# A gather-and-multiply graph layer: leftover rows placed in wider tiles, and the first 128 columns multiplied from a resident tile

## The chip, the cores and the metric

The kernel runs on one core of a Trainium2 chip. The metric is the time of one execution in microseconds (us), measured on the device; lower is better. The engines are named as the profile names them: PE (matmul), PEld (loading of PE's weights), DVE (VectorE), ACT (ScalarE), POOL (GpSimd), SP (SyncE).

## The reference

One layer of a graph network with a residual and a normalisation. The adjacency matrix is sparse in its far columns and nearly full in its first ones, because an entry is present with a probability that falls as the root of both indices.

```python
B, N, F_IN, F_OUT = (8, 4096, 256, 256)
HW = jnp.einsum('bnf,fo->bno', H, W)               # H is x
A_norm = jax.nn.relu((A + A.T) * 0.5)
D = jnp.sum(A_norm, axis=1)
d_inv_sqrt = jnp.where(D > 0, D_safe ** (-0.5), 0.0)
DAD = d_inv_sqrt[:, None] * A_norm * d_inv_sqrt[None, :]
L_norm = jnp.eye(N) - DAD
out = relu(jnp.einsum('nm,bmo->bno', L_norm, HW))
x = _layernorm(x + out, axis=-1)
```

All is float32.

## The kernel before

**First stage (0 to about 584 us).** The adjacency is read in squares of 512 by 512, made symmetric by PE transposes and a DVE addition (`symmetrise`, L364), passed through relu, summed for the degrees (L369) and written to `a_dram`. Beside that, `form` multiplies 128 rows of x by W, scales them and writes them to `g_dram`: a row of `g` has 8 x 256 float32 numbers, 8 KB. The first block of 128 output rows is multiplied densely here (`lead`).

**Second stage (about 584 us to the end).** The other 31 blocks of 128 output rows are worked off in 16 units of two blocks (the last unit has one), in the order `SEQ`. A unit has four quarters of 64 output rows. A column m of the adjacency touches some of the four quarters, which gives a pattern of 1 to 15: bits 1 and 2 are the two quarters of the first block (b=0), bits 4 and 8 those of the second (b=1). Only columns with a pattern above zero have to be fetched. They are sorted into tiles of 128 columns by kind: `KINDS` lists the patterns that have tiles of their own, kind 0 takes all others and whatever finds no place, and multiplies all four quarters. `CAPS[u]` says how many tiles of each kind unit u has. For a tile, `gather` issues two indirect DMAs on POOL: the 128 columns' entries of the adjacency (`ga`, L733, 512 B or 1 KB a row) and the 128 rows of `g` (L744). The `g` tiles go into a ring of `RING` buffers of 1 MB. Slots of a tile that hold no column are left out of the fetch of `g`.

PE multiplies a tile once for each 512-number bank of the output (four banks) and each block that it touches (L933). A product for one quarter uses 64 of PE's columns; two products for different halves stand side by side. `steps_of` therefore puts tiles of kinds 1 and 2, 4 and 8, 5 and 10 into one step, and mixes the (1, 2) steps with those of kind 0.

**The lists.** Which column goes where is computed on the chip, four units ahead. `patterns(u)` finds the pattern of each column (DVE). `count` multiplies by ones and by a triangle on PE, to number the columns of each kind. `place(u)` (L212) takes these numbers from PSUM, keeps those below the kind's capacity and makes slots of them (DVE, tiles of 11 kinds x 32); `place_rest` does so for kind 0. `spread` and `collect` turn slots into lists, `index` turns the lists into the addresses for the gathers. Four units' `place` runs in the first stage, from `count_place`, beside `symmetrise`, and twelve in the second.

**The order around a unit's end.** Work is written in an order made by hand: `after(n, fn)` runs a function n products later, `queue("dve")` and `in_turn` pin an instruction behind the engine's last one. When block b=0 of a unit is complete, `finish` evicts it (ACT, L620, into `y`, one buffer); one product later DVE normalises it (`moments`, `inverse_root`); two products later `lists` puts `count`, `count_rest` and `collect` on PE, into two PSUM banks with the tag `b0`; one later `read(False)` runs on DVE up to the `yield` of `index`, `place_rest` and `place`, and six later `read(True)` the rest. The tag `b0` has four banks, and the next unit's first block needs all four: its third and fourth bank are those that the lists used.

Of the kernel before, what the change touches and what calls it, by code (L numbers as in the profile page):

```python
# [16 lines left out]

KINDS = [1, 2, 3, 0, 6, 9, 5, 10, 12, 4, 8]  # L20

SEQ = [1, 2, 3, 4, 5, 6, 7, 0, *range(8, 16)]

CAPS = [
# [16 lines left out]
]  # L41


# [1 line left out]
def kernel(  # L45
# [36 lines left out]
    Q = 64  # L82
    QU = 4
    HOLD = 10
    RING = 13
    EPS = 1e-5
    NK = len(KINDS)
    tiles = [sum(caps) for caps in CAPS]
    first = [[sum(caps[:k]) for k in range(NK)] for caps in CAPS]
    mid = KINDS.index(0), KINDS.index(12)  # L90
    tmax = max(tiles)

    const = ctx.enter_context(tc.tile_pool(name="const", bufs=1))
# [83 lines left out]
    def patterns(u):  # L177

        used = ipool.tile([P, QU, NB], F32, tag="used", name=f"used_{u}", bufs=1)
        nb = blocks(u)  # L180
        if nb == 1:
            nc.vector.memset(used, 0.0)
        lo = (2 * u + 1) * 2
        nc.vector.tensor_scalar(
            used[:, : 2 * nb],
            part[:, :, lo : lo + 2 * nb].rearrange("p m s -> p s m"),
            0.0,
            None,
            ALU.is_gt,
        )  # L190
# [14 lines left out]
        plan[u] = pat, kind  # L205

    def count(u, tot, low):
        kind = plan[u][1].rearrange("p k m -> p (k m)")
        nc.tensor.matmul(tot, lhsT=ones, rhs=kind, start=True, stop=True)
        nc.tensor.matmul(low, lhsT=lower, rhs=kind, start=True, stop=True)  # L210

    def place(u, tot, low):  # L212

        pat, kind = plan[u]
        pos, _ = scan(tot, low, NK * NB, f"k{u}")
        yield
        pos = pos.rearrange("p (k m) -> p k m", k=NK)  # L220
        fits = ipool.tile([P, NK, NB], F32, tag="fits", name=f"fits_{u}", bufs=1)
        nc.vector.tensor_tensor(
            fits, pos, limit[:, u].unsqueeze(2).to_broadcast([P, NK, NB]), ALU.is_lt
        )
        nc.vector.tensor_tensor(fits, fits, kind, ALU.mult)
# [18 lines left out]
    def place_rest(u, tot, low):  # L244

        slot, rest = plan[u]
        pos, incl = scan(tot, low, NB, f"r{u}")
        yield
        room = CAPS[u][mid[0]] * P
# [3 lines left out]
        nc.vector.scalar_tensor_tensor(  # L253
            pos, pos, float(first[u][mid[0]] * P + 1), fits, ALU.add, ALU.mult
        )
# [47 lines left out]
    def index(u, pl):  # L303
        t = tiles[u]

        low = ipool.tile([P, tmax], F32, tag="low", name=f"low_{u}")
        nc.vector.tensor_copy(low[:, :t], pl[:, 1, :])
        nc.vector.scalar_tensor_tensor(low[:, :t], pl[:, 0, :], float(P), low[:, :t], ALU.mult, ALU.add)
        yield
        gi = ipool.tile([P, tmax], U32, tag="gi", name=f"gi_{u}", bufs=3)  # L310
        nc.vector.tensor_scalar(gi[:, :t], low[:, :t], float(N), None, ALU.add)

        ai = ipool.tile([P, tmax], U32, tag="ai", name=f"ai_{u}", bufs=3)
        m0, m1 = first[u][mid[0]], first[u][mid[1]]
        if blocks(u) == 1:
            m0 = m1 = t
        for ts, n, k in (
            (slice(0, m0), NB, 2 * u + 1),
            (slice(m0, m1), NU, u),
            (slice(m1, t), NB, 2 * u + 2),  # L320
        ):
            if ts.start == ts.stop:
                continue
            nc.vector.tensor_scalar(
                ai[:, ts], low[:, ts], float(n), float(N * n + k), ALU.mult, ALU.add
            )
        plan[u] = gi, ai

    def run(steps):
        for _ in steps:  # L330
# [342 lines left out]
    def targets(u, kind):  # L673

        if kind == 0:
            kind = 15 if blocks(u) == 2 else 3
        out = []
        for b in range(2):
            h = kind >> 2 * b & 3
            if h:  # L680
                out.append((b, {1: slice(0, Q), 2: slice(Q, P), 3: slice(0, P)}[h]))
        return out

    def steps_of(u):
# [12 lines left out]

    with (
# [5 lines left out]
            gath.enter_context(tc.tile_pool(name=f"gath_{k}", bufs=1)).tile([P, G], F32, name=f"g{k}")  # L704
            for k in range(RING)
        ]
        lpool = gath.enter_context(tc.tile_pool(name="spread", bufs=1))
        stat = gath.enter_context(tc.tile_pool(name="stat", bufs=3))
        steps = [(u, step) for u in SEQ for step in steps_of(u)]
# [14 lines left out]
        def gather(n):  # L724

            if n >= len(order):
                return
            u, kind, t = order[n]
            gi, ai = plan[u]
            both = len(targets(u, kind)) == 2  # L730
            at = apool.tile([P, 2 * P], F32, tag="a", name=f"ga_{u}_{t}")
            with queue("pool"):
                nc.gpsimd.indirect_dma_start(  # L733
                    out=at if both else at[:, :P],
# [4 lines left out]
                )  # L739


            gt = ring[n % RING]
            with queue("pool"):
                nc.gpsimd.indirect_dma_start(  # L744
                    out=gt,
# [268 lines left out]
```

## Time and profile before

| | |
|---|---|
| median of 14 runs | 1605.54 us (1599.77 to 1609.9) |
| profiled execution, its own time | 1601.25 us |
| its span, first to last instruction | 1599.5 us |
| granted TensorE clock, mean | 0.981 |
| PE busy | 1493.5 us, 93% |
| DVE busy | 891.6 us, 56% |
| POOL busy | 752.9 us, 47% |
| moved by DMA | 575.71 MB, mean 360 GB/s |

A group of instructions is a line of the kernel, an engine, an operation, what it writes and reads, and the count; then busy time and the mean of one in ns, and the idle time just before, with what ended it. A table of stretches gives for each engine its busy time and the number of its instructions, then the granted clock of PE, the busy share of the DMA engines and their rate.

A float32 product shows as two records, for the weights and for the matmul alike: the 1,576 products of L933 are 3,152 records on PE.

### The profile page before, as it was taken

Reading aid. Unit: us, or ns where it says so; the run is one execution under the profiler, and the core shown is the slowest. Engines: PE = TensorE matmul, PEld = TensorE weight load, DVE = VectorE, ACT = ScalarE, POOL = GpSimd, SP = SyncE. Lnnn points to the kernel's source line nnn. Section 1 sums busy time; section 2 is a strip of 40 time slices with the busy share of each in tenths; the row PEclk is TensorE's granted clock in tenths of the full one; section 3 lists DMA queues with packets and bytes.
Section 4 is the critical chain, followed back from the end, with each engine's and each line's share of the span. In section 5 each row is a group of like instructions: output and inputs, shape, how many; then the busy total and the mean of one; then the engine's idle time right before and its main releaser. Section 6 shows DMA issues by size and latency. Waiting matters only on the chain.

```text
span 1599.5 us, 18959 instructions
## 1 busy us (share of the span) xinstructions
PE 1493.5 (93%) x6544; PEld 778.9 (49%) x6544; DVE 891.6 (56%) x2250; ACT 371.3 (23%) x462; POOL 752.9 (47%) x1109
## 2 busy tenths in 40 slices
PE   6999989998889898999999999899999998999983
PEld 5787877777677643333343333334333332333331
DVE  5675678876474604446384473671176656666542
ACT  3555554554344500101001010010001101100111
POOL 3001010102122257576676676676676667666662
PEclk9999999999999999999999999999999999999998
DMA  9999999999889889999999999999999999999994
GB/s 351 376 362 406 390 374 373 397 383 367 290 325 327 344 351 401 375 404 339 399 370 370 372 369 362 379 367 370 344 351 338 345 376 365 368 387 377 350 342 159
DMA packets 222037, 575.71 MB, mean 360 GB/s; under 512 B 20403, under 2 KB 108771, under 8 KB 184195
## 3 DMA queue, kind: packets, MB, share of 16 engines
q0 software_dynamic: 59552, 316.19, 51.6%
q10 hardware_dynamic: 72032, 134.51, 22.2%
q1 hardware_dynamic: 90352, 123.74, 22.1%
q8 instruction: 54, 0.88, 0.2%
q14 instruction: 47, 0.39, 0.1%
HBM read 479.07 MB, written 136.34 MB: 385 GB/s over the span
## 4 chain that ended last, share of the span: by engine, by line
PE 66%; DMA 18%; issue 6%; DVE 5%; POOL 2%; ACT 2%; another core or an unknown queue 0%; POOLq 0%; ACTq 0%; SPq 0%; DVEq 0%
PE py L933 44%; PE pg L469 10%; DMA g<-g_dram,gi 10%; PE lead L427 5%; DMA a_dram<-sym 4%; PE xtr L458 3%; PE tr L360 3%; DVE sym L364 3%; DMA xin<-in_x_dram 2%; ACT sym L368 1%; DVE part L369 1%; POOL g L744 1%; POOL ga L733 1%; DMA xr<-in_x_dram 1%; DMA adj<-in_adj_dram 1%
## 5 line engine op out<-in xcount | busy, mean ns | idle before, releaser
L933 PE MATMUL py<-g,ga 128*64 128x512 f32 (+1 forms) x3152 | 942.6, 599 | 40.1 <-issue 19.9
L933 PEld LDWEIGHTS py<-g,ga 128*64 128x64 f32 (+1 forms) x3152 | 344.6, 153 | 626.5 <-issue 597.9
L744 POOL DMA_INDIRECT g<-g_dram,gi x302 | 335.7, 1111 | 242.9 <-issue 80.6
L733 POOL DMA_INDIRECT ga<-a_dram,ai x302 | 328.2, 1087 | 99.5 <-issue 86.2
L631 DVE TENSOR_TENSOR xr<-xr,y 128x2048 f32<-128x2048 f32 x31 | 71.2, 2296 | 446.0 <-ACT y L620 388.9
L620 ACT ACTIVATE y<-py,minus_r 128x512 f32<-128x512 f32 x120 | 81.6, 687 | 885.9 <-PE py L933 812.0
L469 PE MATMUL pg<-w_sb,xt 128*128 128x256 f32 x1024 | 230.6, 383 | 5.3 <-ACT xt L459 5.2
L364 DVE TENSOR_TENSOR sym<-tr,adj 128x512 f32<-128x512 f32 x256 | 162.9, 682 | 112.3 <-PE tr L360 95.0
L469 PEld LDWEIGHTS pg<-w_sb,xt 128*128 128x128 f32 x1024 | 194.4, 192 | 33.6 <-ACT xt L459 6.0
L369 DVE TENSOR_REDUCE part<-sym 128x32 f32<-128x2048 f32 x64 | 145.4, 2278 | 63.3 <-ACT sym L368 63.3
L360 PE MATMUL tr<-ident,adj 128*128 128x128 f32 x1024 | 136.0, 283 | 25.3 <-DVE sym L364 12.2
L389 POOL TENSOR_TENSOR r<-e,neg_half 128x4 f32<-128x4 f32 x8 | 8.3, 1039 | 315.8 <-DVE e L388 315.8
L368 ACT ACTIVATE sym<-sym 128x2048 f32<-128x2048 f32 x64 | 122.5, 1915 | 122.2 <-DVE sym L364 122.2
L360 PEld LDWEIGHTS tr<-ident,adj 128*128 128x128 f32 x1024 | 118.4, 145 | 53.3 <-DVE sym L364 24.5
L636 DVE BATCH_NORM_STATS2 stats<-xr 128x6 f32<-128x256 f32 x256 | 87.2, 411 | 19.4 <-POOL xr L631 18.3
L458 PE MATMUL xtr<-ident,xin 128*128 128x128 f32 x512 | 72.5, 286 | 16.4 <-DVE sym L364 14.0
L660 DVE TENSOR_SCALAR xr<-xr,mv,root 128x256 f32<-128x256 f32 x248 | 84.3, 411 | 0.1
L427 PE MATMUL lead<-gt,strip 128*128 128x512 f32 x176 | 82.5, 593 | 0.0
L479 ACT ACTIVATE gt<-pg,r 128x512 f32<-128x512 f32 x88 | 60.5, 687 | 76.8 <-PE pg L469 70.3
L459 ACT COPY xt<-xtr 128x512 f32<-128x512 f32 x128 | 68.4, 590 | 40.9 <-PE xtr L458 39.7
L458 PEld LDWEIGHTS xtr<-ident,xin 128*128 128x128 f32 x512 | 58.6, 145 | 34.3 <-DVE sym L364 26.0
L274 DVE TENSOR_TENSOR hot<-iota_q,at 128x1024 bf16<-128x1024 f32 x64 | 74.1, 1218 | 1.5 <-DMA a_dram<-sym 1.5
(114 smaller groups left out, 579.5 us busy)
## 6 DMA issues: line engine op xcount, KB each, us to landing
adj<-in_adj_dram SPq DMA_DIRECT2D x64, 1024.0 KB
a_dram<-sym ACTq DMA_DIRECT2D x64, 1024.0 KB
xr<-in_x_dram ACTq DMA_DIRECT2D x32, 1024.0 KB
out_dram<-xr SPq DMA_DIRECT2D x31, 1024.0 KB
xin<-in_x_dram SPq DMA_DIRECT2D x44, 512.0 KB
g_dram<-gt ACTq DMA_DIRECT2D x22, 1024.0 KB
xin<-in_x_dram POOLq DMA_DIRECT2D x20, 512.0 KB
g_dram<-held ACTq DMA_DIRECT2D x10, 1024.0 KB
```

The lines of the kernel that those rows point to most:

```text
L360: ins = nc.tensor.transpose(pt[:, c * P : (c + 1) * P], tji[:, c, a * P : (a + 1) * P], ident)
L364: nc.vector.tensor_add(sym[:, a, :], pt, tij[:, a, :])
L368: nc.scalar.activation(sym, sym, AF.Relu, scale=0.5)
L369: nc.vector.tensor_reduce(part[:, i * A : (i + 1) * A, j * S // Q : (j + 1) * S // Q], sym.rearrange("p a (c q) -> p a c q", q=Q), AX.X, A ...
L427: nc.tensor.matmul(lead[c], lhsT=strip, rhs=g[:, c * S : (c + 1) * S], start=not done, stop=len(done) == NB - 1, skip_group_check=True,)
L458: nc.tensor.transpose(pt[:, k, c, :], xin[b // H][:, b % H + k, c * P : (c + 1) * P], ident)
L469: ins = nc.tensor.matmul(pg[:, k * FO : (k + 1) * FO], lhsT=xt[:, b + k, c, :], rhs=w_sb[:, c, :], start=(c == 0), stop=(c == FC - 1),)
L636: nc.vector.bn_stats(stats[:, b, :], z[:, b, :])
L660: nc.vector.tensor_scalar(z[:, b, :], z[:, b, :], mv[:, b, 0:1], rstd[:, b : b + 1], ALU.subtract, ALU.mult,)
L733: nc.gpsimd.indirect_dma_start(out=at if both else at[:, :P], out_offset=None, in_=a_pairs if both else a_rows, in_offset=bass.IndirectOff ...
L744: nc.gpsimd.indirect_dma_start(out=gt, out_offset=None, in_=g_dram, in_offset=bass.IndirectOffsetOnAxis(ap=gi[:, t : t + 1], axis=0), boun ...
L933: last_product = nc.tensor.matmul(py[2 * u + 1 + b][c][rows, :], lhsT=at[:, off + rows.start : off + rows.stop], rhs=gt[:, c * S : (c + 1) ...
```

## The change

Two things are done at once.

1. A column of kind 1, 2, 4 or 8 (one quarter) that finds no place in the tiles of its kind is offered free places in tiles of two quarters, in three rounds (`OFFERS`): first kinds 3 and 12, then 5 and 10, then 9 and 6. Only what is left after that goes to kind 0. `place` computes for every kind how far each round reaches (`upto`) and by how much the slot number is shifted there (`off`, `step`, `way`). `KINDS` is put in another order, so that one slice serves two kinds, and `CAPS` has new numbers.
2. In the eleven units of `HUB` the first 128 columns take no part in the lists. They are a step of their own, multiplied for all four quarters from a tile `hub` that holds rows 0 to 127 of `g` and is loaded once; their adjacency entries come by a plain DMA. The ring has 12 buffers in place of 13.

In `index` the `yield` moves from before the address computations to behind them.

```diff
-KINDS = [1, 2, 3, 0, 6, 9, 5, 10, 12, 4, 8]
+KINDS = [3, 1, 2, 4, 8, 12, 5, 10, 9, 6, 0]
+ONE = slice(1, 5)
+OFFERS = [
+    (0, (1, 4), (3, 12)),
+    (0, (2, 8), (3, 12)),
+    (1, (1, 2), (5, 10)),
+    (1, (4, 8), (5, 10)),
+    (2, (1, 2), (9, 6)),
+    (2, (4,), (6,)),
+    (2, (8,), (9,)),
+]
+HUB = {0, 1, 3, 6, *range(8, 15)}
 CAPS = [
-    [4, 3, 2, 7, 1, 2, 2, 1, 1, 3, 3],
+    [2, 3, 3, 3, 2, 1, 2, 1, 2, 1, 6],
...
-    [3, 3, 1, 1, 1, 1, 1, 1, 1, 3, 3],
+    [1, 2, 2, 2, 2, 1, 1, 1, 1, 1, 1],
...
-    RING = 13
+    RING = 12
...
     def patterns(u):
...
+        if u in HUB:
+            nc.vector.memset(pat[:, :1], 0.0)
...
     def place(u, tot, low):
         pat, kind = plan[u]
-        pos, _ = scan(tot, low, NK * NB, f"k{u}")
+        pos, incl = scan(tot, low, NK * NB, f"k{u}")
         yield
         pos = pos.rearrange("p (k m) -> p k m", k=NK)
+        n = ONE.stop - ONE.start
+        nc.vector.tensor_copy(total, incl.rearrange("p (k m) -> p k m", k=NK)[:, :, NB - 1])
+        nc.vector.tensor_tensor(free, total, limit[:, u], ALU.min)
+        nc.vector.tensor_add(free, free, base[:, u])
+        nc.vector.tensor_tensor(total, total, limit[:, u], ALU.max)
+        nc.vector.tensor_add(ends, base[:, u], limit[:, u])
+        nc.vector.tensor_copy(upto[:, 0], limit[:, u, ONE])
+        nc.vector.tensor_copy(off[:, 0], base[:, u, ONE])
+        for s, ones_, twos in OFFERS:
+            k, t = at_once(*ones_), at_once(*twos)
+            c = slice(k.start - ONE.start, k.stop - ONE.start, k.step)
+            nc.vector.tensor_sub(off[:, s + 1, c], free[:, t], upto[:, s, c])
+            nc.vector.tensor_sub(upto[:, s + 1, c], ends[:, t], off[:, s + 1, c])
+            nc.vector.tensor_tensor(upto[:, s + 1, c], upto[:, s + 1, c], total[:, k], ALU.min)
+            nc.vector.tensor_add(free[:, t], upto[:, s + 1, c], off[:, s + 1, c])
+        nc.vector.tensor_copy(upper, limit[:, u])
+        nc.vector.tensor_copy(upper[:, ONE], upto[:, 3])
         nc.vector.tensor_tensor(
-            fits, pos, limit[:, u].unsqueeze(2).to_broadcast([P, NK, NB]), ALU.is_lt
+            fits, pos, upper.unsqueeze(2).to_broadcast([P, NK, NB]), ALU.is_lt
         )
+        nc.vector.tensor_sub(step, off[:, 1:], off[:, :3])
+        for s in range(3):
+            more = way if s == 0 else ipool.tile([P, QU, NB], F32, tag="used", name=f"more_{u}_{s}", bufs=1)
+            nc.vector.tensor_tensor(
+                more, pos[:, ONE], upto[:, s].unsqueeze(2).to_broadcast([P, n, NB]), ALU.is_ge
+            )
+            nc.vector.tensor_tensor(
+                more, more, step[:, s].unsqueeze(2).to_broadcast([P, n, NB]), ALU.mult
+            )
+            if s > 0:
+                nc.vector.tensor_add(way, way, more)
+        nc.vector.tensor_add(pos[:, ONE], pos[:, ONE], way)
...
     def index(u, pl):
...
-        yield
         gi = ipool.tile([P, tmax], U32, tag="gi", name=f"gi_{u}", bufs=3)
...
         plan[u] = gi, ai
+        yield
...
         few, all_rows = groups[:2]
+        all_rows += [[(0, -1)]] * (u in HUB)
...
         def gather(n):
...
+            if t < 0:
+                if not hub_loads:
+                    with queue("pool"):
+                        hub_loads.append(nc.gpsimd.dma_start(hub, g_dram[:P, :]))
+                with queue("pool"):
+                    nc.gpsimd.dma_start(at, a_dram[:P, (2 * u + 1) * P : (2 * u + 3) * P])
+                got[u, t] = (at, hub)
+                return
...
+            n = len(ring_tiles)
             gt = ring[n % RING]
+            ring_tiles.append(gt)
```

More of the change, by code (lines that the diff above doesn't have):

```diff
@@ L89 @@
     first = [[sum(caps[:k]) for k in range(NK)] for caps in CAPS]
-    mid = KINDS.index(0), KINDS.index(12)
+    mid = KINDS.index(4), KINDS.index(5)
     tmax = max(tiles)
@@ L210, in count, with at_once @@
         nc.tensor.matmul(low, lhsT=lower, rhs=kind, start=True, stop=True)
+    def at_once(*kinds):
+        at = [KINDS.index(k) for k in kinds]
+        return slice(at[0], at[-1] + 1, at[-1] - at[0] or 1)
     def place(u, tot, low):
         pat, kind = plan[u]
-        pos, _ = scan(tot, low, NK * NB, f"k{u}")
+        pos, incl = scan(tot, low, NK * NB, f"k{u}")
         yield
         pos = pos.rearrange("p (k m) -> p k m", k=NK)
+        n = ONE.stop - ONE.start
+        total = ipool.tile([P, NK], F32, tag="total", name=f"total_{u}", bufs=1)
+        nc.vector.tensor_copy(total, incl.rearrange("p (k m) -> p k m", k=NK)[:, :, NB - 1])
+        free = ipool.tile([P, NK], F32, tag="free", name=f"free_{u}", bufs=1)
+        nc.vector.tensor_tensor(free, total, limit[:, u], ALU.min)
+        nc.vector.tensor_add(free, free, base[:, u])
+        nc.vector.tensor_tensor(total, total, limit[:, u], ALU.max)
+        ends = ipool.tile([P, NK], F32, tag="ends", name=f"ends_{u}", bufs=1)
+        nc.vector.tensor_add(ends, base[:, u], limit[:, u])
+        upto = ipool.tile([P, 4, n], F32, tag="upto", name=f"upto_{u}", bufs=1)
+        nc.vector.tensor_copy(upto[:, 0], limit[:, u, ONE])
+        off = ipool.tile([P, 4, n], F32, tag="off", name=f"off_{u}", bufs=1)
+        nc.vector.tensor_copy(off[:, 0], base[:, u, ONE])
[6 more added lines that the diff above has]
+            nc.vector.tensor_add(free[:, t], upto[:, s + 1, c], off[:, s + 1, c])
+        upper = ipool.tile([P, NK], F32, tag="upper", name=f"upper_{u}", bufs=1)
+        nc.vector.tensor_copy(upper, limit[:, u])
+        nc.vector.tensor_copy(upper[:, ONE], upto[:, 3])
@@ L221, in place @@
         fits = ipool.tile([P, NK, NB], F32, tag="fits", name=f"fits_{u}", bufs=1)
         nc.vector.tensor_tensor(
-            fits, pos, limit[:, u].unsqueeze(2).to_broadcast([P, NK, NB]), ALU.is_lt
+            fits, pos, upper.unsqueeze(2).to_broadcast([P, NK, NB]), ALU.is_lt
         )
+        step = ipool.tile([P, 3, n], F32, tag="step", name=f"step_{u}", bufs=1)
+        nc.vector.tensor_sub(step, off[:, 1:], off[:, :3])
+        way = ipool.tile([P, n, NB], F32, tag="way", name=f"way_{u}", bufs=1)
@@ L248, in place_rest @@
         yield
-        room = CAPS[u][mid[0]] * P
+        room = CAPS[u][KINDS.index(0)] * P
         nc.vector.tensor_scalar(over[:, u : u + 1], incl[:, NB - 1 : NB], float(room), None, ALU.is_gt)
@@ L253, in place_rest @@
         nc.vector.scalar_tensor_tensor(
-            pos, pos, float(first[u][mid[0]] * P + 1), fits, ALU.add, ALU.mult
+            pos, pos, float(first[u][KINDS.index(0)] * P + 1), fits, ALU.add, ALU.mult
         )
@@ L318, in index @@
             (slice(0, m0), NB, 2 * u + 1),
-            (slice(m0, m1), NU, u),
-            (slice(m1, t), NB, 2 * u + 2),
+            (slice(m0, m1), NB, 2 * u + 2),
+            (slice(m1, t), NU, u),
         ):
@@ L706 @@
         ]
+        hub = gath.enter_context(tc.tile_pool(name="hub", bufs=1)).tile([P, G], F32, name="g_hub")
+        hub_loads = []
+        ring_tiles = []
         lpool = gath.enter_context(tc.tile_pool(name="spread", bufs=1))
@@ L728, in gather @@
             u, kind, t = order[n]
+            both = len(targets(u, kind)) == 2
+            at = apool.tile([P, 2 * P], F32, tag="a", name=f"ga_{u}_{t % tmax}")
+            if t < 0:
[6 more added lines that the diff above has]
+                return
             gi, ai = plan[u]
-            both = len(targets(u, kind)) == 2
-            at = apool.tile([P, 2 * P], F32, tag="a", name=f"ga_{u}_{t}")
             with queue("pool"):
```

28 rows, old and new, of the table CAPS are left out of this document.

## The prediction

> **What bounds the kernel now.** I read the page's head first, then the chain of work that ended last, then the stretches cut at the units' ends, then the groups of instructions, and last the order of time around one unit's end.
>
> ```profile
> PE 1493.5 (93%) x6544; PEld 778.9 (49%) x6544; DVE 891.6 (56%) x2250; ACT 371.3 (23%) x462; POOL 752.9 (47%) x1109
> ...
> PE 66%; DMA 18%; issue 6%; DVE 5%; POOL 2%; ACT 2%; another core or an unknown queue 0%; POOLq 0%; ACTq 0%; SPq 0%; DVEq 0%
> ...
> 0.00:584.00 584.00, 535.97 (x2896) 418.57 (x2898) 362.07 (x529) 282.05 (x330) 91.38 (x508) 0.98 0.97 360
> 584.00:1582.00 998.00, 957.53 (x3650) 360.35 (x3646) 523.97 (x1701) 84.56 (x125) 655.88 (x596) 0.99 0.97 365
> ```
>
> The second stage takes 998 of 1599.5 us; PE is busy for 957.5 us of it and the DMA engines are 97% busy at 365 GB/s. So two resources are nearly full, and DVE (524 us) and POOL (656 us) are not.
>
> How long PE needs for a step is seen from the weight loads and from the evictions of a last step:
>
> ```profile
> 1267.47 0.14 PEld L933 LDWEIGHTS py<-g,ga 128*64 128x64 f32 x2 [0.29 <-issue]
> 1267.90 0.14 PEld L933 LDWEIGHTS py<-g,ga 128*64 128x64 f32 x2 [0.28 <-issue]
> 1478.88 0.69 ACT L620 ACTIVATE y<-py,minus_r 128x512 f32<-128x512 f32 x1 [31.93 <-PE py L933]
> 1481.46 0.69 ACT L620 ACTIVATE y<-py,minus_r 128x512 f32<-128x512 f32 x1 [0.17 <-PE py L933]
> ```
>
> Two 64-column loads go in every 0.43 us, so a pair of halves costs what one full product costs: 2 x 0.43 us for a bank. The first and fourth bank of a step are evicted 2.58 us apart, 0.86 us a bank. I call one step's worth for four banks a slot: 3.44 us.
>
> **The slots and the bytes.** From `CAPS` and `steps_of`, a (1, 2), (4, 8), (5, 10) step counts as many slots as its fuller half has products, kinds 3 and 12 one, a kind 0 or hub tile two (one in the unit with a single block). Before there are 259 slots in 302 tiles; after, 250 slots in 268 gathered tiles and 11 hub steps. By unit in the order worked: before 23, 20, 18, 17, 16, 16, 15, 31, 15, 14, 15, 14, 14, 13, 13, 5; after 23, 19, 18, 16, 15, 15, 14, 30, 15, 14, 14, 13, 13, 13, 13, 5. That is 9 x 3.44 = 31.0 us less of PE.
>
> ```profile
> 927.35 0.31 PE L209 MATMUL lists<-kind,ones 128*128 128x352 bf16 x1
> 928.59 1.94 PE L933 MATMUL py<-g,ga 128*64 128x512 f32 x8
> 930.00:934.00 4.00, 4.00 (x22) 1.37 (x20) 2.60 (x18) 0.00 (x0) 3.09 (x4) 1.00 1.02 392
> 938.00:942.00 4.00, 2.89 (x9) 0.88 (x11) 3.72 (x20) 0.00 (x0) 1.66 (x3) 1.00 1.00 410
> ```
>
> The 259 slots are 891 us of the 998; the lists' products, 1.24 us in each of 14 units, 17 us more; 90 us are waits. Where the DMA engines are full they move some 400 GB/s.
>
> The bytes: I counted the patterns of the reference's adjacency. Before, 33,471 rows of `g` are fetched in 38,656 slots of tiles; after, 32,174 in 34,304. In both cases the columns left over fit in kind 0, so the dense way at the kernel's end is not taken. The hub takes 1,297 rows of 8 KB out, 10.6 MB; its own load adds 1.05 MB; the `ga` rows fall from 25.8 to 25.0 MB. So 10.4 MB less, and at the 365 GB/s above 28.5 us.
>
> PE's 31.0 and the DMA's 28.5 us do not add: they are the same time seen from two nearly full resources. Per unit I took the larger of slots x 3.44 us + 1.24 us and bytes at 400 GB/s, with 4.2 MB for a unit's x and output. Before it gives 946 us, after 919 us: units 1, 3 and 0 are set by PE, the rest within 10% by either. I take -28 us.
>
> **Tail and ring.** At the end PE waits for gathers although the DMA is not full:
>
> ```profile
> 1552.00:1582.00 30.00, 21.08 (x70) 6.77 (x70) 11.35 (x42) 2.50 (x5) 11.96 (x11) 1.00 0.70 271
> 1571.10 4.61 PE L933 MATMUL py<-g,ga 128*64 128x512 f32 x16 [2.50 <-DMA g<-g_dram,gi]
> 1564.61 13.23 DMA g<-g_dram,gi
> ```
>
> A gather lands 13 us after its issue, a ring buffer comes free only when PE is done with it, and the last (4, 8) and (1, 2) steps use two tiles in 3.44 us. Before, the last such run is 6 + 9 tiles against 13 buffers; after, 4 + 9 against 12, and a hub step, which needs no ring buffer, lets the gathers run ahead by 6.9 us earlier in that unit. I take -4 us (bounds 0, the ring being shorter, and -9, the PE idle of that stretch). In all the second stage's tiles give **-32 us** (-20 to -40).
>
> POOL issues 34 tiles fewer, 34 x 2.2 us, and 12 plain DMAs more:
>
> ```profile
> L744 POOL DMA_INDIRECT g<-g_dram,gi x302 | 335.7, 1111 | 242.9 <-issue 80.6
> L733 POOL DMA_INDIRECT ga<-a_dram,ai x302 | 328.2, 1087 | 99.5 <-issue 86.2
> L417 POOL DMA_DIRECT2D xin<-in_x_dram x20 | 15.2, 760 | 102.3 <-PE xtr L458 101.6 <-issue 0.7
> ```
>
> That is -75 + 9 us on an engine with 342 us free in the stage: nothing by itself.
>
> **The price: DVE.** `place` grows by 38 operations on 1 to 12 numbers a partition (7 ahead of the offers, 7 x 4 in them, 3 behind) and 9 on 4 x 32.
>
> ```profile
> 931.12 0.17 DVE L653 TENSOR_TENSOR half<-root 128x8 f32<-128x8 f32 x1
> 931.32 0.17 DVE L654 SCALAR_TENSOR_TENSOR half<-half,rstd 128x8 f32<-128x8 f32 x1
> L225 DVE TENSOR_TENSOR fits<-fits,kind 128x352 f32<-128x352 f32 x16 | 8.4, 523 | 0.5
> L173 DVE TENSOR_TENSOR pos_r<-incl_r,lists 128x32 f32<-128x32 f32 x13 | 2.4, 187 | 0.5
> ```
>
> Small dependent ones start 0.20 us apart: 38 x 0.20 = 7.6 us. Between 187 ns for 32 numbers and 523 for 352, 128 cost about 0.29 us: 9 x 0.29 = 2.6 us. So 10.2 us for each unit, 163 us in all, on an engine that is not the bound on average. Where it falls decides.
>
> *First stage.* Four `place` run in two pairs beside `symmetrise`, with nothing in the code that pins their order there:
>
> ```profile
> 239.00:271.00 32.00, 28.14 (x41) 1.00 1.01 364
> 271.00:304.00 33.00, 25.83 (x55) 1.00 1.04 396
> 304.00:340.00 36.00, 30.86 (x55) 1.00 1.02 381
> 340.00:380.00 40.00, 27.50 (x47) 0.91 1.04 405
> ...
> 243.82 0.69 DVE L364 TENSOR_TENSOR sym<-tr,adj 128x512 f32<-128x512 f32 x1
> 244.43 0.52 DVE L222 TENSOR_TENSOR fits<-pos_k,limit 128x352 f32<-128x352 f32 x1
> 244.86 0.68 DVE L364 TENSOR_TENSOR sym<-tr,adj 128x512 f32<-128x512 f32 x1
> ```
>
> The first four rows show DVE alone (busy, instructions), then clock, DMA share and rate. The two stretches that hold the pairs have 3.9 and 5.1 us of DVE idle for 20.4 us more each; those behind have 7.2 and 12.5. If all idle time is filled, 20.4 - 11.1 and 20.4 - 17.6 are left over: 12 us. If none is, 41 us. PE's transposes wait for the additions that DVE then does later, PSUM having four banks for them, and the DMA, full at 1.02, cannot make up more than the few loads buffered. I take **+20 us**: nearer to the filled end, since the present `place` is interleaved with the additions one by one, as the last three rows show.
>
> *Second stage.* Here DVE waits once a unit, for the next eviction:
>
> ```profile
> 1229.00:1278.00 49.00, 49.00 (x223) 17.89 (x221) 34.98 (x114) 6.83 (x11) 34.16 (x31) 1.00 0.96 349
> 1263.05 2.29 DVE L631 TENSOR_TENSOR xr<-xr,y 128x2048 f32<-128x2048 f32 x1 [12.38 <-ACT y L620]
> 1273.50 0.52 DVE L174 TENSOR_TENSOR pos_k<-pos_k,lists 128x352 f32<-128x352 f32 x1
> 1276.62 0.30 DVE L324 TENSOR_SCALAR ai<-low 128x6 uint32<-128x6 f32 x3
> 1321.51 2.29 DVE L631 TENSOR_TENSOR xr<-xr,y 128x2048 f32<-128x2048 f32 x1 [21.07 <-ACT y L620]
> ```
>
> 12.4 and 21.1 us of idle cover 10.2, in units of 14 and 15 slots; the cover is gone where a unit with `place` has 13 slots. The other cover is at the unit's end. The first block's last product ends 0.7 us, one eviction, ahead of the addition at 1263.05; `place` has read its banks at 1274.0, 11.7 us later, and the moved `yield` puts the 0.3 us of the addresses and one operation of `gi` ahead of that: 12.2 us. PE comes to those banks after what is left of block b=1, the lists, and two banks of the next step. That was 4 slots + 1.24 + 1.7 = 16.7 us and becomes 13.3 us, with 3 slots, in seven of the twelve units that have `place`, and 9.8 us, with 2, in unit 11, where PE waits 2.4 us. In the seven it just suffices, and any lateness of DVE is then PE's. I take **+3 us** (0 to 25: twelve units late by 2 us).
>
> **Sum.** -32 + 20 + 3 = -9 us on the profiled execution's 1601.25 us. That lies 4.3 us under the median of the runs, so against 1605.5 it is 1596.5 us.
>
> **The rivals.**
>
> 1. *DVE in the first stage costs in full, and the end is slower.* Each place round then lasts as long as DVE's work in it: 4 x 10.2 = 41 us. With -32 and +3 that is +12 us: 1617 us. For it: DVE has 9 us free where 41 are added. Against: 20 us of idle right behind. It decides from 29 us on. Chance 0.25.
> 2. *DVE's saturation at the units' ends.* Twelve units, each with 2 us of PE's wait, are +24 instead of +3, so +12 in all: 1617 us. For it: 13.3 against 12.2 us. Against: DVE still has idle time in units of 14 slots and more. Chance 0.12.
> 3. *The lists cost nothing that lasts.* The first stage's additions find room, because PE or the DMA is awaited there anyway: 0 to +8 for the price, -32 for the tiles: 1578 us. Chance 0.23.
> 4. *DVE holds POOL, and the gathers come late.* POOL's issues are stretched where DVE reads two operands:
>
> ```profile
> 613.53 2.29 DVE L631 TENSOR_TENSOR xr<-xr,y 128x2048 f32<-128x2048 f32 x1 [57.09 <-issue]
> 613.61 3.09 POOL L744 DMA_INDIRECT g<-g_dram,gi  x1 [1.20 <-remote]
> L744 POOL DMA_INDIRECT g<-g_dram,gi x302: 999/1005/3089, 572.1 to 1564.6; - x151
> L733 POOL DMA_INDIRECT ga<-a_dram,ai x302: 940/944/3040, 567.1 to 1562.3; - x151
> ```
>
> One issue took 3.09 us where the median (the middle of each three) is 1.005. Mean less median, 0.106 and 0.143 us, times 302 each is 75 us of hold under 524 us of DVE; 122 us more of DVE would hold POOL 17 us more. If all of it falls where a gather is awaited, -9 + 17 = +8: 1613 us. Against: POOL has 342 us free. Chance 0.10. [...]
>
> The forecast itself, faster by 2 to 20 us, has 0.30.
>
> **How the numbers follow.** The forecast and rival 3 hold 0.53; with the ends of the others that pass zero, faster by over 0.2% (3.2 us, about what the runs can tell) gets 0.56, within it 0.14, slower 0.30. The range takes the tiles at their better end with rival 3's price, -40 + 8 + 0 = -32, and reaches 5 us past the slower rivals' +12: 1573 to 1622 us. The likeliest case alone is 1586 to 1603.
>
> **What would show it.** Second stage: 3,048 records of L933 instead of 3,152, `g` gathers 268, the stage some 25 to 33 us shorter, rate near 365 GB/s still. First stage: its end moves from 584 to about 604 us, with DVE full and PE with gaps from 239 to 340 us. At the units' ends, PE's waits for `pos_k` stay under 1 us. The prediction is wrong if the first stage ends within 8 us of before, if it ends later than 620 us, or if the second stage is not over 15 us shorter.

## The result and the profile after

| | before | after |
|---|---|---|
| median | 1605.69 us (47 runs) | 1536.44 us (10 runs, 1531.63 to 1546.99) |
| ratio | | 0.9576, 95% interval 0.9558 to 0.9595 |
| span of the profiled execution | 1599.5 us | 1527.6 us |
| lead's first eviction | 581.28 us | 593.87 us |
| second stage (584.0 to 1582.0, and 596.5 to 1513.8) | 998 us | 917 us |

Faster by 69 us where 9 were forecast: the sign was right, and the time lies below the range, which began at 1573 us. The page of the changed kernel, engines and then the chain that ended last:

```profile
PE 1444.7 (95%) x6440; PEld 763.7 (50%) x6440; DVE 984.4 (64%) x3013; ACT 369.6 (24%) x462; POOL 693.7 (45%) x1053
...
PE 70%; DMA 14%; DVE 8%; issue 4%; POOL 2%; ACT 2%; POOLq 0%; ACTq 0%; DVEq 0%; SPq 0%
```

The stretches of its two stages and of its last 30 us of products (PE, PEld, DVE, ACT, POOL busy; clock; DMA share; GB/s):

```profile
0.00:596.50 596.50, 543.36 (x2896) 424.37 (x2898) 381.11 (x719) 281.47 (x330) 94.15 (x509) 0.97 0.96 353
596.50:1513.80 917.30, 901.37 (x3546) 339.35 (x3544) 597.89 (x2274) 83.80 (x125) 594.27 (x540) 1.00 0.99 385
1483.80:1513.80 30.00, 23.47 (x84) 7.30 (x80) 14.36 (x52) 5.50 (x8) 10.38 (x10) 1.00 0.72 274
```

The first stage is 12.5 us longer and the second 81 us shorter; what follows it is 4 us shorter, 17.5 and 13.8 us. The slots (9 x 3.44 = 31 us) do not explain 81. With 250 slots (860 us) and the lists (17 us), 40 us of the second stage are left over where the kernel before had 90. And the DMA engines, 97% busy at 365 GB/s before, are 99% busy at 385 GB/s. The queue that carries the gathers, in that stage of the kernel before (packets, MB, share of the 16 engines' time):

```profile
DMA packets 119565, 364.31 MB, mean 365 GB/s; under 512 B 15571, under 2 KB 80083, under 8 KB 86307
...
q0 software_dynamic: 53990, 297.55, 77.5%
```

and of the changed kernel:

```profile
DMA packets 114193, 352.70 MB, mean 385 GB/s; under 512 B 11718, under 2 KB 76230, under 8 KB 82246
...
q0 software_dynamic: 48614, 285.91, 78.3%
```

A megabyte of gathers kept the 16 engines for 0.775 x 998 / 297.55 = 2.60 us before and 0.783 x 917.3 / 285.91 = 2.51 us after. So the same engines, about as busy, moved more. Why is what the experiments had to find.

### The profile page after: what moved, and what is told of

Read it like the earlier page. It is cut to its first block, busy times and chain, and to the rows that moved or that the text cites. A ratio compares the mean times of both kernels' runs of the same rounds, so it can differ in the third digit from the quotient of the medians.

```text
span 1527.6 us, 19342 instructions
## 1 busy us (share of the span) xinstructions
PE 1444.7 (95%) x6440; PEld 763.7 (50%) x6440; DVE 984.4 (64%) x3013; ACT 369.6 (24%) x462; POOL 693.7 (45%) x1053
## 4 chain that ended last, share of the span: by engine, by line
PE 70%; DMA 14%; DVE 8%; issue 4%; POOL 2%; ACT 2%; POOLq 0%; ACTq 0%; DVEq 0%; SPq 0%
PE py L1008 50%; PE pg L530 9%; DMA g<-g_dram,gi 7%; PE lead L488 5%; DMA a_dram<-sym 4%; PE tr L421 3%; DVE sym L425 3%; DMA xin<-in_x_dram 3%; PE xtr L519 3%; DVE part L430 2%; ACT sym L429 1%; PE lists L356 1%; POOL limit L165 0%; POOL base L166 0%; ACT xt L520 0%
## 5 line engine op out<-in xcount | busy, mean ns | idle before, releaser
L1008 PE MATMUL py<-g,ga 128*64 128x512 f32 (+1 forms) x2872 | 811.5, 596 | 15.2 <-DMA g<-g_dram,gi 12.6
L1008 PEld LDWEIGHTS py<-g,ga 128*64 128x64 f32 (+1 forms) x2872 | 290.7, 150 | 522.5 <-issue 496.7
L819 POOL DMA_INDIRECT g<-g_dram,gi x268 | 303.4, 1132 | 215.3 <-issue 73.8
L806 POOL DMA_INDIRECT ga<-a_dram,ai x268 | 292.2, 1090 | 106.1 <-issue 72.7
L421 PE MATMUL tr<-ident,adj 128*128 128x128 f32 x1024 | 139.5, 287 | 30.3 <-DVE sym L425 18.4
L1008 PE MATMUL py<-g_hub,ga 128*128 128x512 f32 x176 | 78.3, 597 | 0.0
```

The costliest lines, as they stand in the source:

```text
L421: ins = nc.tensor.transpose(pt[:, c * P : (c + 1) * P], tji[:, c, a * P : (a + 1) * P], ident)
L806: nc.gpsimd.indirect_dma_start(out=at if both else at[:, :P], out_offset=None, in_=a_pairs if both else a_rows, in_offset=bass.IndirectOff ...
L819: nc.gpsimd.indirect_dma_start(out=gt, out_offset=None, in_=g_dram, in_offset=bass.IndirectOffsetOnAxis(ap=gi[:, t : t + 1], axis=0), boun ...
L1008: last_product = nc.tensor.matmul(py[2 * u + 1 + b][c][rows, :], lhsT=at[:, off + rows.start : off + rows.stop], rhs=gt[:, c * S : (c + 1) ...
```

## The experiments

I name a run's second stage by one row: from the lead's last eviction to 13.8 us before the end. For the kernel before that is

```profile
584.00:1585.70 1001.70, 957.53 (x3650) 360.35 (x3646) 527.42 (x1710) 84.88 (x125) 659.38 (x599) 0.99 0.97 364
```

so 1002 us in place of the 998 above. The kernel before ran beside every experiment, and a ratio compares runs of one session. Its median was between 1593 and 1606 us from session to session, so traces of different sessions can differ by some 10 us that no edit made.

The first theories were these. *POOL*: 34 gathers fewer free POOL. *Bytes*: the stage lasts as long as its DMA. *Lead*: a hub step lets the gathers run ahead.

**The hub tile alone.** The old lists and capacities, hub steps in seven units whose kind 0 loses a tile, 12 ring tiles.

```diff
+HUB = {0, 1, 3, 6, 10, 11, 12}
...
-    RING = 13
+    RING = 12
...
```

> The kernel before with the hub tile alone, in seven units (0, 1, 3, 6, 10, 11, 12, those whose kind 0 can give up a tile), ring of 12, the old lists and place. Slots stay 259; 295 gathered tiles instead of 302; about 6 MB less. Theory POOL (PE's waits in the second stage come from POOL, which needs 2.55 us to issue a tile's two gathers, too slow for units with under 2.9 us of PE per tile): 7 tiles less, 18 us of POOL, so -8 to -15 us: about 1594 us. Theory bytes (the DMA's 365 GB/s are the limit): 6 MB, -16 us: about 1590 us. Theory lead (a step that needs no gather lets the ring fill, which removes the waits): most of the 50 us of waits that the change took away go here too, -30 or more: 1575 us or less. All: the first stage ends at 584 us as before.

```profile
586.90:1582.70 995.80, 955.95 (x3650) 357.19 (x3646) 525.99 (x1713) 84.96 (x125) 652.28 (x592) 0.99 0.95 360
```

1599.15 us, ratio 0.9971 (0.9951 to 0.9991): 5 us of the 69, although 6 MB went. That is less than any of the three theories said.

**The offers and capacities alone.** The new code without the hub, a kind 0 tile more in its eleven units: 250 slots, 279 tiles, all 33,471 rows.

```diff
-HUB = {0, 1, 3, 6, *range(8, 15)}
+HUB = set()
...
-    RING = 12
+    RING = 13
...
```

> The changed kernel without the hub: the eleven hub steps are kind 0 tiles again (one more in each of those units), ring of 13. Slots 250 as in the changed kernel, 279 gathered tiles, the rows of g as before (33,471). Theory POOL: 1.116 tiles a slot, half way between before (1.166) and after (1.072), so half of the 50 us of waits goes: 1605 - 31 - 25 + 12 = about 1561 us. Theory bytes: no bytes saved, so PE's 31 us turn into waits: 1605 - 3 + 12 = about 1612 us. Theory lead: the waits stay, 1605 - 31 + 12 = about 1586 us. All: first stage ends near 597 us.

```profile
596.30:1530.30 934.00, 908.90 (x3546) 340.64 (x3542) 598.56 (x2266) 83.80 (x125) 609.70 (x551) 0.99 0.99 388
```

1544.54 us, ratio 0.9644 (0.9607 to 0.968), faster than any of the three theories said. The DMA's rate goes up to 388 GB/s with nearly all the bytes kept: the offers bring most of it, and the lead of the gathers is not the cause.

**The bytes put back**, as plain copies by SP, one for each unit.

```diff
+            nc.sync.dma_start(copied, g_dram[u * 80 : (u + 1) * 80, :])
```

> The changed kernel with 10.5 MB more to move in the second stage: each of the 16 units copies 80 rows of g_dram (0.66 MB) to a scratch in DRAM by one DMA issued from SP. That gives back the bytes that the change saved and leaves POOL, PE and the ring as they are. Theory bytes: +27 us, about 1563 us. Theories POOL and lead: under +6 us, about 1537 to 1542 us.

Its second stage:

```profile
617.70:1536.10 918.40, 905.05 (x3546) 339.40 (x3542) 597.56 (x2275) 84.42 (x125) 587.80 (x541) 0.99 0.99 384
```

What the DMA moved in it:

```profile
DMA packets 114215, 352.88 MB, mean 384 GB/s; under 512 B 11718, under 2 KB 76230, under 8 KB 82246
```

1550.87 us, ratio 0.9691 (0.9652 to 0.9731). The unchanged stage looks like proof against the bytes. The last row shows otherwise: the stage moved 352.88 MB, as without the copies. SP had issued them in the first stage, whose end went to 615 us. The run says nothing on the second stage.

**POOL's time put back.** Three small fills ahead of each gather of `g`.

```diff
+            for _ in range(3):
+                with queue("pool"):
+                    nc.gpsimd.memset(hold, 0.0)
```

> The changed kernel with three memsets of 128x1 on POOL ahead of each tile's gathers (about 0.3 us for each of 268 tiles, 80 us of POOL in all): that gives back the POOL time of the 34 tiles that the change saved. Bytes, slots and ring stay. Theory POOL: the waits come back, +25 to +50 us, 1560 to 1585 us. Theories bytes and lead: under +6 us.

```profile
597.50:1525.10 927.60, 909.18 (x3546) 343.80 (x3546) 602.24 (x2275) 84.35 (x125) 694.59 (x1344) 0.99 0.99 384
```

1541.52 us, ratio 0.962 (0.9597 to 0.9644): 100 us more of POOL in the stage cost it 10 us by the two traces, 7 us by the ratios. POOL is not where 50 us went.

**The old capacities in the new code.** 259 slots, 302 tiles, no hub.

> The changed code with the old capacities, no hub tile and 13 ring tiles: 259 slots and 302 tiles again, but the new order of kinds, the new place with its offers in DVE (nothing is offered that the old code did not place, as the old capacities hold all) and the moved turn of the generator. Theory numbers (the gain of the changed kernel comes from the new capacities alone, fewer slots and fewer two-tile steps; the new code costs some 12 us in the first stage): about 1605 + 12 = 1617 us, the waits of PE in the second stage 80 to 95 us as before. Theory code (the order in which the new place, the turn and the kinds fall out is what took PE's waits from 90 to 40 us): 1605 + 12 - 50 = about 1567 us, waits near 40 to 50 us.

```profile
598.50:1596.40 997.90, 959.56 (x3650) 357.93 (x3646) 602.68 (x2274) 84.39 (x125) 662.35 (x598) 0.99 0.96 365
```

1611.52 us, ratio 1.0068 (1.0045 to 1.0091). The code by itself costs 11 us, and the first stage is where it is longer; the second is as before, at 365 GB/s again. The gain is in the numbers.

**A third of the second tiles not fetched.** The kernel before with 34 gathers of `g` left out; PE multiplies what the tile held.

```diff
+        left_out = {n for n, m in list(enumerate(second))[RING:] if m and sum(second[:n]) % 3 == 0}
...
+            if n in left_out:
+                got[u, t] = (at, gt)
+                return
```

> The kernel before with 34 of its 302 gathers of g left out, every third of those that fill the second tile of a step (PE multiplies what the ring tile still holds, so the output is another one); slots, lists, steps and the gathers of a stay as they are. 268 gathers of g are left, as many as the changed kernel has. Theory supply (PE's 90 us of waits in the second stage come from gathers of g, which arrive later than the two-tile steps want them): the waits fall by 35 to 55 us, 1605 - 45 = about 1560 us. Theory slots (the waits hang on the list work and on the steps' order and not on how many tiles of g are wanted): 1595 to 1605 us, with 259 slots as before.

```profile
585.00:1531.50 946.50, 935.81 (x3650) 356.66 (x3646) 524.45 (x1703) 84.84 (x125) 627.14 (x562) 0.99 0.94 354
```

1546.11 us, ratio 0.9645 (0.9605 to 0.9684), with all 259 slots. The waits hang on the supply, at the upper end of that theory's 35 to 55 us. This run took away gathers, bytes and waits together; the next two part them.

**The same 34 issued, but with no row to fetch**, and **34 plain copies of 0.85 MB in their places**, awaited by nobody.

```diff
+            rows = none if n in left_out else gi[:, t : t + 1]
```
```diff
+                    nc.gpsimd.dma_start(copied[m : m + 104, :], g_dram[m : m + 104, :])
```

> The kernel before with the same 34 gathers of g still issued by POOL and still waited for, but with an index list that names no row, so that they move nothing (PE multiplies what the tile held; the output is another one). 302 gathers, 28.9 MB less. Theory bytes (the kernel before was held by what the DMA engines can move while PE wants it, and the 1546 us of the run without these gathers came from 28.9 MB less): about 1546 us, within 6. Theory count (each gather costs its place in POOL's queue and in the ring, whatever it moves): 1590 to 1605 us. In between, both.

> The kernel before with the same 34 gathers of g replaced at their places in POOL's queue by plain copies of 104 rows of g from DRAM to DRAM, 0.85 MB each: POOL's instructions and the 28.9 MB stay, but the tile is neither waited for by PE nor does the copy wait for a ring tile (PE multiplies what the tile held; the output is another one). Theory bytes: 1595 to 1610 us, as before, with the waits of PE back at 80 to 95 us. Theory ring (a gather must wait until PE gives the ring tile back and then needs 13 us to land; 34 fewer of them let the others start sooner): 1545 to 1565 us.

Their second stages, without rows and then with copies:

```profile
585.50:1519.90 934.40, 928.17 (x3650) 348.83 (x3646) 526.28 (x1711) 85.80 (x125) 662.35 (x599) 1.00 0.96 359
```
```profile
587.60:1564.10 976.50, 949.75 (x3650) 362.60 (x3646) 525.52 (x1705) 85.73 (x125) 633.45 (x598) 0.99 0.97 373
```

Without rows 1534.52 us, ratio 0.9621 (0.9606 to 0.9636); with copies 1579.09 us, ratio 0.9904 (0.9888 to 0.9919). The number of gathers costs nothing; what they move does. The copies missed both theories: the bytes are all back, but only 42 of the 67 us that the stage had lost (44.6 of 60.5 us by the medians, which are of one session).

**The steps unmixed.** `mixed = few + all_rows`.

> The changed kernel with the steps of a unit's first two groups one after the other (all the two-tile steps of quarters 1 and 2 first, then the steps of all rows and the hub's), not alternating. Same tiles, slots and bytes. Theory bursts (PE waits where several two-tile steps follow each other, since a step takes two tiles in one slot of 3.44 us and a gather brings one in some 2.6 to 2.75 us): each unit has some three such steps in a row, about 1 us late each when the ring has run short, +15 to +40 us: 1552 to 1577 us. Theory mean (only the mean number of tiles per slot matters, since 12 tiles in the ring level out a few steps): within 5 us of the changed kernel, 1532 to 1542 us.

1531.99 us, ratio 0.9585 (0.9543 to 0.9626): no effect that the interval shows, and bursts of two-tile steps are out.

**Units 1 to 4 as of old**, twice, the second time beside the changed kernel.

```diff
+EARLY = {1, 2, 3, 4}
...
+        offers = u not in EARLY
...
```

> The changed kernel, but units 1 to 4, whose lists are made in the first stage, keep their old capacities and the old place without offers: 252 slots and 273 tiles in place of 250 and 268. Theory offers (the 12.6 us by which the first stage ends later come from the offers' instructions on DVE): the first stage ends 8 to 12 us sooner (the lead's first eviction at 582 to 586 us and not at 594), the second stage takes 7 us more for two slots and up to 10 for five tiles more: 1534 to 1545 us. Rival (the first stage is longer for another reason, the order of the code or the hub's load): the first stage stays near 594 us and the time goes to 1543 to 1555 us.

> The changed kernel with the old capacities and the old place in units 1 to 4, once more, beside the changed kernel itself on the same chip. Its first stage ended 11 us sooner in the run before this and it has 2 slots and 5 tiles more (7 us of PE): 3 to 5 us faster than the changed kernel (ratio to before about 0.955) if these two are all; no difference (0.957) if the sooner end of the first stage is given back in waits.

> The changed kernel itself, for the comparison on one chip: 1531 to 1540 us, ratio 0.956 to 0.960, PE's waits in the second stage 35 to 50 us. If its waits in a second trace are above 65 us, the 40 us of the first were luck of one execution.

The lead's first eviction, here and in the changed kernel:

```profile
582.53 0.69 ACT L688 ACTIVATE y<-lead,minus_r 128x512 f32<-128x512 f32 x1 [21.19 <-PE lead L495]
```
```profile
593.87 0.69 ACT L681 ACTIVATE y<-lead,minus_r 128x512 f32<-128x512 f32 x1 [21.87 <-PE lead L488]
```

The first stage ends 11 us sooner, so its 12.6 us are the offers of these four units. The time hardly follows: 1528.61 us, ratio 0.9551 (0.9508 to 0.9594), then 0.9579 (0.9564 to 0.9594) beside 0.9593 (0.9573 to 0.9613) for the changed kernel, which the intervals do not part. The second stage takes 6 to 13 us more. The changed kernel's second trace has a second stage of 918 us, so the 917 us were not the luck of one execution.

**The rows of a tile in another order.** A column's number within its tile was its partition, so the rows missing from a partly filled tile are always the last partitions. Here row r goes to partition 17 r mod 128, in the kernel before and in the changed one. Tiles, slots, bytes and gathers stay.

```diff
+        nc.vector.tensor_scalar(ip, ip, 17.0, None, ALU.mult)
         nc.vector.tensor_single_scalar(digit, ip, P - 1, ALU.bitwise_and)
```

> The kernel before with the rows of each tile laid out in another order: row r of a tile goes to partition 17 r mod 128 and not to partition r, so that the rows that a partly filled tile lacks are spread over its partitions instead of being its last ones. Same tiles, slots, bytes and gathers; two small instructions of 32 elements more or less per unit. Theory uneven (the tiles of the kernel before are 87% full and their missing rows are always the last partitions; if each DMA engine serves a fixed block of partitions, the engines of the first partitions carry more and the others idle: the DMA's 97% and 364 GB/s against 99% and 385 GB/s in the changed kernel, whose tiles are 94% full): 1550 to 1575 us. Rival even (which partitions are missing makes no difference to the DMA engines): 1597 to 1606 us.

The kernel before in that order, its stage, then the gathers' queue in it:

```profile
586.40:1537.30 950.90, 933.24 (x3650) 351.01 (x3646) 527.87 (x1723) 85.81 (x126) 664.98 (x598) 1.00 0.99 383
```
```profile
DMA packets 119506, 363.86 MB, mean 383 GB/s; under 512 B 15569, under 2 KB 80081, under 8 KB 86304
...
q0 software_dynamic: 53930, 297.08, 79.2%
```

1551.79 us, ratio 0.9728 (0.9699 to 0.9757). The same 364 MB and as many packets, 51 us less, at 383 and not 365 GB/s. The two traces are of different sessions; beside each other in one session the medians are 1593.34 and 1551.79 us. So where the missing rows lie is worth 42 to 51 us.

> The changed kernel with the same order of rows in its tiles. Theory uneven: its tiles are 94% full, so less is to be had, 5 to 15 us: 1515 to 1528 us. Rival even: 1528 to 1540 us, as the changed kernel.

> The changed kernel with the order of rows 17 r mod 128, beside the one above on the same chip: 1506 to 1514 us, ratio 0.944 to 0.950.

```profile
598.10:1495.40 897.30, 894.38 (x3546) 336.00 (x3542) 597.72 (x2287) 85.83 (x125) 601.67 (x540) 1.00 1.00 393
```
```profile
q0 software_dynamic: 48616, 285.92, 78.7%
```

The second stage in the second session's trace:

```profile
599.20:1508.70 909.50, 900.70 (x3546) 337.15 (x3544) 600.44 (x2288) 83.51 (x125) 603.79 (x540) 0.99 0.99 387
```

1510.06 us, ratio 0.9473 (0.9441 to 0.9505), and in a second session 1523.34 us, 0.9497 (0.9472 to 0.9521). Beside the changed kernel's 917 and 918 us the second stage is 20 us shorter in the first of these traces and 8 in the second; by the ratios, 0.9576 and 0.9593 without this order, the whole gains 13 to 19 us. That is less than in the kernel before, as is to be expected where the tiles are fuller (32,174 rows in 34,304 slots, 94%, against 33,471 in 38,656, 87%).

**The bytes put back where they count.** The changed kernel with 10.8 MB of copies on POOL's queue, behind every eighth gather.

```diff
+            if n % 8 == 7:
+                m = n // 8 * 40
+                with queue("pool"):
+                    nc.gpsimd.dma_start(copied[m : m + 40, :], g_dram[m : m + 40, :])
```

> The changed kernel with 10.8 MB of plain copies from DRAM to DRAM put on POOL's queue behind every eighth gather of g (33 copies of 40 rows), so that they run in the second stage and not, as those of the earlier run turned out to do, in the first (its second stage moved 352.88 MB and the changed kernel's 352.68). Theory bytes (the second stage of the changed kernel is as long as its DMA engines need: 99% busy at 385 GB/s): 10.8 MB at 385 GB/s are 28 us: 1555 to 1565 us. Rival (the DMA has room and PE is the bound): 1530 to 1542 us.

```profile
598.00:1536.70 938.70, 910.75 (x3546) 345.50 (x3542) 595.86 (x2274) 85.81 (x125) 614.39 (x573) 1.00 1.00 388
```

1553.35 us, ratio 0.9742 (0.9714 to 0.9771): 21 us in the stage for 10.8 MB, or 27 us by the ratios, where 28 would be the full price of the bytes at 385 GB/s. The changed kernel's second stage is held, for the most part, by what its DMA engines move.

**Two more versions**: units 1 to 4 as of old with 17 r, and the changed kernel with 7 r.

> The changed kernel with the order of rows 17 r mod 128 in its tiles and with the old capacities and the old place in units 1 to 4. If the two add: the first stage ends some 11 us sooner, two slots and 1.2 MB more are 3 to 7 us: 1502 to 1508 us. Rival: no better than the order of rows alone, since units 1 to 4 need more bytes: 1508 to 1515 us.

> The changed kernel with row r of a tile on partition 7 r mod 128 in place of 17 r mod 128. [...] Rival (the stage with 17 r is as good as even already): 0.946 to 0.951.

1521.54 us, ratio 0.9485 (0.9459 to 0.951), and 1510.89 us, 0.9478 (0.946 to 0.9496). Neither can be told from 17 r alone: that the two changes of the first add does not show, and the second is no faster than 17 r's 0.9473 and 0.9497. With 7 r the second stage is 897.3 us, as in the shorter trace with 17 r, 20 us above PE's slots and lists (860 and 17 us).

## Why the prediction was wrong

**What the stage lasts.** Shown is that the layout costs time, 42 to 51 us in the kernel before and 8 to 20 in the changed one. That missing rows which lie together leave some of the DMA engines with less to do is the theory behind these runs; which engine serves which partition no trace here shows, so what each of them carries is not known. What can be counted is the rows that the tiles lack: 38,656 - 33,471 = 5,185 before, 279 x 128 - 33,471 = 2,241 with the offers alone, 34,304 - 32,174 = 2,130 after. The stages, with the difference to the kernel before:

| | measured stage |
|---|---|
| before | 1002 us |
| old capacities in the new code | 998 (-4) |
| hub alone | 996 (-6) |
| offers alone | 934 (-68) |
| units 1 to 4 as of old, two traces | 930 (-72), 924 (-78) |
| after, two traces | 917 (-84), 918 (-83) |
| before, 17 r | 951 (-51) |
| units 1 to 4 as of old, 17 r | 921 (-81) |
| after, 17 r, two traces | 897 (-104), 909 (-92) |
| after, 7 r | 897 (-104) |

Traces of different sessions can differ by some 10 us. The order of rows is worth more where more rows are missing, 42 to 51 us with 5,185 of them and 8 to 20 with 2,130. That 34 copies, which have no missing rows, restored only 42 of the 67 us fits as well.

Against it seems to stand the mean share of the 16 engines, 97% in the kernel before: the other 3% are 30 us and not 51. But packets overlap, and the share adds them up: in the packet records of that trace more than 16 packets run at once for 27% of the second stage, which hides the moments with fewer. Those moments can be counted. From 8 to 13 packets run at once for 10.4% of the stage in the kernel before and for 2.9% in the other row order; for 4.7% in the changed kernel and for 2.0% with the order. So some engines had nothing to do while others worked, and the order took most of that away.

It is not the whole of the 51 us. On the mean of the engines, time without a packet, counted from the moments with fewer than 16 at once, fell by some 25 us, from 55 to 30, and time in packets by some 22, from 967 to 945. For the gathers alone a MB took 2.60 us of the engines' time and then 0.792 x 950.9 / 297.08 = 2.535 us; in the changed kernel 2.51, and with the order 0.787 x 897.3 / 285.92 = 2.47. Why packets are shorter where the rows are spread stays open. One rival is untested: the order also changes which rows of `g` are read near each other in time.

**By its steps.**

- *Slots, 259 to 250*: right, 3,048 records on PE (2,872 of ring tiles and 176 of the hub) and 268 gathers.
- *Tiles, -32 us*: this is the step that failed; the second stage measured -81. The larger of PE and bytes at 400 GB/s, unit by unit, gave 946 us before and 919 after. After is 917, but before is 998, and the 52 us that the sum did not reach were carried over as if they stayed. They were the sign of a resource not priced: DMA engines 97% busy at 365 GB/s that moved over 400 in other places. With the rows apart the same tiles and bytes take 951 us, so 42 to 51 of the 52 us were the layout's, and the changed kernel's fuller tiles took away more than half of that. "10.4 MB less" priced the bytes alone and not the 5,185 - 2,130 = 3,055 missing rows that went as well. The forecast "rate near 365 GB/s still" was wrong with it.
- *Tail, -4*: PE is busy for 23.47 of the last 30 us and not 21.08: -2.4.
- *POOL, nothing*: right within 10 us, by the fills put back.
- *First stage, +20 (12 to 41)*: +12.6 by the lead's eviction, at the lower end. The cause is the named one, since without these offers it is gone. DVE's price was too high: 984.4 - 891.6 = 92.8 us more busy time for 16 units, 5.8 each, and not 10.2. The 38 small operations were priced one behind the other, 0.20 us apart; where two do not depend on each other, the trace has them 0.08 us apart (the changed kernel's L249 at 264.94 and L250 at 265.02 us).
- *Second-stage DVE, +3*: right within what the traces tell. The old capacities in the new code give the same stage as before, and PE's products wait 2.0 us for `pos_k`, once, by the first of these groups of the changed kernel; under 1 us was foretold.

```profile
L1008 PE MATMUL py<-g,ga 128*64 128x512 f32 (+1 forms) x2872 | 811.5, 596 | 15.2 <-DMA g<-g_dram,gi 12.6 <-DVE pos_k L188 2.0 <-issue 0.3
...
L819 POOL DMA_INDIRECT g<-g_dram,gi x268 | 303.4, 1132 | 215.3 <-issue 73.8 <-PE py L1008 61.8 <-DMA g<-g_dram,gi 54.0
...
L1008 PE MATMUL py<-g_hub,ga 128*128 128x512 f32 x176 | 78.3, 597 | 0.0
```

*The rivals.* First-stage DVE in full (1617 us): no, 12.6 and not 41. DVE at the units' ends: no. Lists that cost nothing (1578): nearest, but for another reason. POOL held: no; 122 us more of DVE were feared, 74 came, and POOL's gathers take 1,132 ns on the mean as against 1,111. The long issues themselves are in the trace of the kernel before: of its 604 gather issues 72 took over 1.2 us, all beside a DVE operation with two operands (TENSOR_TENSOR and its variants), and of the 368 beside none the longest took 1.19 us.

**The account.** Second stage -84.4: with the rows apart the two kernels, in one session, differ by 950.9 - 897.3 = 53.6 us, and the layout's loss falls from 50.8 to 20.0 us, by 30.8. Of the 53.6, the 11.2 MB less of gathers at 383 GB/s would be 29; the other 25 go with 31 us less of PE. This split is argued, not measured. With the first stage's +12.6 that is -72, as the spans have it. By medians and ratios, which hold the sessions apart, it is 42 us with the rows apart (1551.79 - 1510.06) and some 23 to 29 us for the layout.

The sign was right, and the fewer slots and bytes that gave it have their part in the gain; the size was not, because the layout was in no term and in no rival. Of the three signs of being wrong none came: for the second stage only a gain that is too small had been named.

## What to carry to other kernels

A sum that leaves a twentieth of a stage unexplained must not carry the rest over as a constant: ask what would remove it. For gathers with missing rows, count the missing rows and not the bytes alone, ask on which partitions they lie, and try to spread them; here one more instruction per unit took 42 to 51 us from the kernel before, and with the change it gives the fastest version, at 0.947 to 0.950 of the time before. And look in the trace when a put-back transfer really ran before reading anything from it.

## What the hardware showed that was not expected

- A DMA share of 97% left room: the same bytes took 51 us less at 99% (42 us by the medians of one session) when only the partitions of the missing rows changed. The share adds up packets that overlap, more than 16 at once for 27% of that stage.
- A gather that fetches no row cost nothing measurable: the ratio was 0.9621 (0.9606 to 0.9636) with 34 of them and 0.9645 (0.9605 to 0.9684) without them.
